# Graph attention layer on one core: the turned source ids leave PSUM through ScalarE instead of VectorE, and ScalarE instead of SyncE issues their way to DRAM

## The chip, the cores and the metric

The kernel runs on one core of one Trainium2 chip. The metric is the device time of one execution in microseconds (us), measured as the median of several runs. Engines are named as the profile names them: PE is TensorE, PEld its weight loads, DVE VectorE, ACT ScalarE, POOL GpSimd, SP SyncE. A q behind a name (SPq, ACTq) marks instructions of the engine's sequencer, such as the issue of a DMA.

## What is computed

A graph attention layer over 12,500 nodes with 128 features and 412,500 edges, whose targets are sorted. In the reference's terms (`src` and `dst` are the two rows of `edge_index`; the layer attends from `src` to `dst` and sums at `src`):

```
h, q, k, v = x@Wn+bn, x@Wq+bq, x@Wk+bk, x@Wv+bv;  eh = edge_attr@We+be
hmid   = leaky_relu(concat(q[src], k[dst], eh) @ A1 + b1, 0.2)
scores = leaky_relu(hmid @ A2 + b2, 0.2)
w      = softmax(scores.mean(-1), axis=0)          # over all edges
out    = segment_sum(w[:, None] * v[dst], src)
y      = gamma * layernorm(h + out) + beta
result = layernorm(x + y)
```

## The kernel before, in words

The edges arrive sorted by target, but the sums are by source, so the kernel sorts them by source on the chip, through DRAM. It has two kinds of work, which are interleaved in one written-out order.

**Making records** (`make`, lines 797 to 1020). The 403 groups of 1024 edges are cut into six parts. For each group PE multiplies one-hot matrices with rows of a key and value table (`rows`, L914 and L919), ACT takes the result out of PSUM into a record tile `rec` (L929, and L930 adds the source id within its block), and POOL scatters it to a table `rtab` in DRAM, with eight indirect DMAs a group (L941). There are six buffers for `rec`. Two tables `rtab` alternate between parts.

**Summing records** (`sums_of`, lines 1072 to 1407). When a part's records are all written, its 49 units, of two blocks of source nodes each and 14 or 12 tiles of 128 edges, are worked off while the next part is made: 294 units in all. The last part's units run with nothing left to make. The steps of one unit that matter here, with their lines:

- `load` (L1109): SP loads the unit's records, `rt`, 1.6 to 1.8 MB.
- `sources` (L1131): DVE reads the source ids out of `rt` into `sl`, a column for each tile.
- `turn` (L1139): PE turns `sl` into rows, into a PSUM tile named `psc`. There is one buffer of this name, and `scores` uses it too.
- `turned` (L1146): DVE takes the turned ids out of PSUM into bytes, `slT` (12 or 14 partitions of 128), clamping negative ones to 0.
- `put` (L1153): SP writes `slT` to a small DRAM tile `row` (1.5 or 1.8 KB).
- `spread` (L1158): SP reads `row` back, repeated over all 128 partitions, into `rowB`.
- `load_q` (L1120): SP loads the query rows `qs`.
- `onehot` (L1170): DVE compares `rowB` with each partition's number: the one-hot matrix `ohT`, in three or four pieces a unit.
- `hidden` (L1184, L1193), `sloped` (L1204, ACT) and `leaky` (L1208, DVE): the hidden layer `hm`; ACT writes the sloped copy and DVE takes the larger of the two.
- `scores` (L1221, PE, into `psc`), `above_zero` (L1235, ACT, a Relu out of PSUM into `z`), `heads` (L1247, PE), `maxima` (L1257, L1262, DVE), `maximum` (L1268, PE), `reference` (L1276, L1277, DVE).
- `weights` (L1286, ACT, needs `ref` of L1277), `select` (L1295, DVE), `weigh` (L1309, ACT, one instruction for a tile), `add` (L1338, PE).
- `lowered` (L1328, L1331, ACT), `before_it` (L1319, SP, loads `old`), `total` (L1354, DVE), `store` (L1361, SP, writes `atab`).

Nothing is scheduled by a planner at this point: `lags` and `last_lags` (lines 1044 to 1070) give for every step how many steps after the unit's own start it is recorded, and each engine executes its instructions in the recorded order. `turned` and `put` stand at the same step, two after `turn`; `spread` stands three steps later. An engine that waits for one instruction holds back everything behind it. SP also issues, in the same recorded order, the loads of the making part: `eat` (L808), `dstb` (L810), `kvs` (L826).

After the last unit a closing stage normalises the rows (lines 1410 to 1613).

Of the kernel before, what the change touches and what calls it, by code (L numbers as in the profile page):

```python
# [15 lines left out]
AF = mybir.ActivationFunctionType  # L16
ALU = mybir.AluOpType
# [4 lines left out]
P = 128  # L22
# [433 lines left out]
def sorted_path(  # L456
# [8 lines left out]
    nc = tc.nc  # L465
# [34 lines left out]
    for j, part in enumerate((1.0, -1.0)):  # L500
        nc.vector.tensor_scalar(
            A2s[:, H + 1 + j : H + 2 + j], A2s[:, H : H + 1], part * SLOPE / (1 - SLOPE), None,
            op0=ALU.mult,
# [6 lines left out]
    for j, part in enumerate((1.0, -1.0)):  # L510
        nc.vector.tensor_scalar(
            b2_r[:, H + 1 + j : H + 2 + j], b2_r[:, H : H + 1], part * SLOPE / (1 - SLOPE), None,
            op0=ALU.mult,
# [10 lines left out]
        out=signs, in_=signs, compare_op=ALU.not_equal, fill=SLOPE - 1, base=-(H + 2),  # L524
# [190 lines left out]
    def spans():  # L715
# [24 lines left out]
        out=above, in_=above, compare_op=ALU.is_gt, fill=0.0, base=0,  # L740
# [331 lines left out]
    def sums_of(bp):  # L1072
# [3 lines left out]
        for p, bs, t in units:  # L1076
            nt = len(bs) * t
# [65 lines left out]
        def turned(i):  # L1143
            st, nt = state[i], plans[i][0]
            st["slT"] = scp.tile([TM, P], U8, name="slT")
            nc.vector.tensor_scalar(  # L1146
                st["slT"][:nt, :], st.pop("pT")[:nt, :P], 0.0, None, op0=ALU.max
            )

        def put(i):  # L1150
            st, nt = state[i], plans[i][0]
            st["row"] = srow.tile([TM, P], U8, name="row")
            nc.sync.dma_start(out=st["row"][:nt, :], in_=st.pop("slT")[:nt, :])  # L1153

        def spread(i):
            st, nt = state[i], plans[i][0]
# [215 lines left out]
        for i, (nt, nk, s0, load_at, o) in enumerate(plans):  # L1372
            do(load_at, load, i)
            do(s0 + o["sources"], sources, i)
            do(s0 + o["turn"], turn, i)
            do(s0 + o["turned"], turned, i)
            do(s0 + o["turned"], put, i)
            do(s0 + o["spread"], spread, i)
            do(s0 + o["q"], load_q, i)
            for k, (c, c1) in enumerate(pieces(i)):  # L1380
                n, s = c1 - c, s0 + 2 * k
                do(s + o["onehot"], onehot, i, c, n, k)
                do(s, hidden, i, c, c, n, k)
                do(s + o["sloped"], sloped, i, c, c, n, k, late=1)
                do(s + o["leaky"], leaky, i, c, c, n, k, late=1)
            do(s0 + o["scores"], scores, i, 0, nt)
            do(s0 + o["above"], above_zero, i)
            do(s0 + o["heads"], heads, i, 0, nt)
            do(s0 + o["maxima"], maxima, i)
            do(s0 + o["maximum"], maximum, i, late=1)  # L1390
            do(s0 + o["reference"], reference, i)
            do(s0 + o["weights"], weights, i)
            do(s0 + o["old"], before_it, i)
            do(s0 + o["lowered"], lowered, i)
            for j, t0 in enumerate(range(0, nt, 4)):
                n = min(4, nt - t0)
                do(s0 + o["select"] + 2 * j, select, i, t0, n)
                do(s0 + o["weigh"] + 2 * j, weigh, i, t0, n)
                do(s0 + o["add"] + 2 * j, add, i, t0, n)
            do(s0 + o["total"], total, i)  # L1400
            do(s0 + o["store"], store, i)
# [328 lines left out]
    with tc.manual_schedule():  # L1730
        done = 0
        for p in range(NP + 1):
# [32 lines left out]
            tabs, made, nt = tables() if p == 0 else iter(()), 0, 1 + (2 * ng - 1) * (NB + 7) + ng  # L1765
# [99 lines left out]
```

## Time and profile before

| | us |
|---|---|
| median of 3 runs | 4985.54 (4974.44 to 4991.73) |
| the profiled execution | 4977.97 |
| its span, first to last instruction | 4976.3 |
| first and last `slT` (L1146) | 765.0 and 4810.6 |
| last indirect DMA of the records (L941) | 4395.4 |

The profiled execution is 7.6 us below the median; what lies around its span is 1.7 us. Four stretches are told apart in what follows, by what runs in them: up to 765 us the tables and the first part's records are made and no unit runs; from 765 to 3000 and from 3000 to 4396 units and records are interleaved; from 4396 to 4830 only the last part's units run; then the closing stage.

Wait rows read "engine, line waited for: total us, how often, the longest". A wait of several semaphores is put down to the one that came last by the profile. Rows of a window table give, for a stretch, its length and for each engine its busy time and instructions, then PE's granted clock, the share of the DMA engines and GB/s.

### The profile page before, as it was taken

The numbers are of one execution on the slowest core, as the hardware profiler recorded it, in microseconds if no ns is written. First come the engines' busy times: TensorE is split into PE (matmuls) and PEld (weight loads), VectorE is DVE, ScalarE is ACT, GpSimd is POOL, SyncE is SP. The second block draws the span as 40 slices with busy tenths as digits, with TensorE's granted clock in tenths as the row PEclk, the third lists the DMA queues.
The fourth block names the chain that finished last, engine by engine and source line by source line (L and its number), as shares of the span: only waits on it lengthen the run. The fifth ranks groups of instructions, "written<-read, shape, count | busy, mean of one in ns | idle before, by whom it ended". The sixth has DMA issues, their size and how long they took to land. (4 is left out here: it accounts for less than half of the span.)

```text
span 4976.3 us, 87101 instructions
## 1 busy us (share of the span) xinstructions
PE 4076.9 (82%) x27267; PEld 3176.9 (64%) x27568; DVE 4181.3 (84%) x9010; ACT 3168.0 (64%) x8326; POOL 3327.3 (67%) x3280
## 2 busy tenths in 40 slices
PE   3665547878888989988988888988889888889997
PEld 2444435666666766776766676776667666666786
DVE  7888867888888888888988887888889898877777
ACT  2442224655656777777777776777777666667785
POOL 3777777777777777777777777767667777731003
PEclk7787868999999999999999999999999999999999
DMA  5888978999888998888898888888888898889864
GB/s 187 285 288 272 369 246 300 317 318 307 275 280 295 315 310 308 311 307 299 315 308 310 303 310 280 306 303 307 297 297 302 300 312 304 298 289 308 302 238 171
DMA packets 603263, 1462.23 MB, mean 294 GB/s; under 512 B 103678, under 2 KB 329105, under 8 KB 600996
## 3 DMA queue, kind: packets, MB, share of 16 engines
q1 hardware_dynamic: 447696, 1027.15, 62.9%
q0 software_dynamic: 154752, 429.39, 22.7%
q8 instruction: 220, 3.60, 0.3%
q14 instruction: 255, 2.09, 0.1%
q10 hardware_dynamic: 340, 0.01, 0.0%
HBM read 884.13 MB, written 585.06 MB: 295 GB/s over the span
## 5 line engine op out<-in xcount | busy, mean ns | idle before, releaser
L941 POOL DMA_INDIRECT rtab<-rec,idx x3224 | 3242.7, 1006 | 1150.6 <-issue 783.3
L929 ACT ACTIVATE rec<-pkv 128x1024 f32<-128x1024 f32 x806 | 821.6, 1019 | 1162.7 <-PE pkv L919 519.1
L1309 ACT ACTIVATE ohw<-ohs,w 128x128 f32<-128x128 bf16 x3822 | 1256.1, 399 | 121.8 <-DVE ohs L1295 59.0
L1338 PE MATMUL psm<-rt,ohw 128*128 128x128 f32 x7644 | 1085.4, 285 | 3.4 <-ACT ohw L1309 0.8
L1338 PEld LDWEIGHTS psm<-rt,ohw 128*128 128x128 f32 x7644 | 997.7, 197 | 101.4 <-ACT hm L1204 13.0
L919 PE MATMUL pkv<-WeS,eat 128*128 128x256 f32 x3224 | 920.5, 412 | 0.0
L1208 DVE TENSOR_TENSOR hm<-ph,hm 128x512 f32<-128x512 f32 (+1 forms) x1029 | 662.5, 644 | 265.9 <-ACT hm L1204 261.2
L914 PE MATMUL pkv<-kvs,ohd 128*128 128x256 bf16 x3224 | 530.0, 291 | 290.5 <-ACT rec L929 283.0
L1184 PE MATMUL ph<-ident,rt 128*128 128x128 f32 x3822 | 625.4, 284 | 118.1 <-DVE hm L1208 112.9
L1170 DVE TENSOR_SCALAR ohT<-rowB,iotaP,power 128x512 bf16<-128x512 uint8 (+2 forms) x1176 | 598.0, 519 | 93.0 <-DMA rowB<-row 92.7
L914 PEld LDWEIGHTS <-ohd 128*128 128x128 bf16 x3224 | 317.0, 103 | 540.6 <-issue 423.4
L919 PEld LDWEIGHTS pkv<-WeS,eat 128*128 128x128 f32 x3224 | 606.4, 209 | 70.2
L1184 PEld LDWEIGHTS ph<-ident,rt 128*128 128x128 f32 x3822 | 442.2, 146 | 323.9 <-issue 144.9
L1204 ACT ACTIVATE hm<-ph 128x512 f32<-128x512 f32 (+1 forms) x1029 | 567.0, 551 | 33.8 <-PE ph L1193 26.8
L857 DVE TENSOR_SCALAR ohd<-dstb,node 128x1152 bf16<-128x1152 uint8 x404 | 564.9, 1398 | 0.0
L1193 PE MATMUL ph<-ohT,qs 128*128 128x512 bf16 (+2 forms) x2051 | 531.6, 340 | 29.2 <-DVE ohT L1170 14.5
L883 DVE TENSOR_TENSOR ats<-pc,oh 128x792 f32<-128x792 f32 x403 | 391.1, 970 | 37.1 <-PE pc L865 37.1
L1221 PE MATMUL psc<-hm,A2s 128*32 128x384 f32 (+2 forms) x2352 | 360.0, 550 | 63.1 <-DVE hm L1208 34.4
L1295 DVE TENSOR_TENSOR ohs<-iotaE,sl 128x512 bf16<-128x512 bf16 (+1 forms) x1029 | 409.1, 398 | 1.0 <-ACT ohw L1309 1.0
L847 DVE TENSOR_REDUCE few<-oh 128x99 bf16<-128x792 bf16 x403 | 395.1, 980 | 13.9
L894 DVE TENSOR_REDUCE pos<-ats 128x8 f32<-128x792 f32 x403 | 389.1, 966 | 1.7
L1247 PE MATMUL psm<-headsum,z 128*128 128x4 f32 (+1 forms) x2058 | 256.7, 245 | 58.0 <-DVE part L1354 50.8
(192 smaller groups left out, 3876.2 us busy)
## 6 DMA issues: line engine op xcount, KB each, us to landing
rt<-rtab SPq DMA_DIRECT2D x147, 1820.0 KB
rt<-rtab SPq DMA_DIRECT2D x147, 1560.0 KB
eat<-in_ea SPq DMA_DIRECT2D x201, 512.0 KB
rtab<-rec,idx POOLq DMA_INDIRECT x3224
dstb<-dtab SPq DMA_DIRECT2D x201, 256.0 KB
rtab<-empty SPq DMA_DIRECT2D x76, 520.0 KB
qs<-qtab SPq DMA_DIRECT2D x294, 128.0 KB
atab<-part SPq DMA_DIRECT2D x294, 128.0 KB
```

The costliest lines, as they stand in the source:

```text
L857: nc.vector.tensor_scalar(to, ids[:, cols], node, None, op0=ALU.is_equal)
L914: nc.tensor.matmul(pk[:, i, h, :], ohd[t], kvs, start=(h == 0), stop=False,)
L919: nc.tensor.matmul(pk[:, i, :, :D], eat[:, (j + i) * P : (j + i + 1) * P], WeS, start=False, stop=True,)
L929: nc.scalar.activation(rec[:, :, :, : 2 * D], pk, AF.Copy)
L941: one_tile = nc.gpsimd.indirect_dma_start(out=rtab[p % TABS][:, :], out_offset=bass.IndirectOffsetOnAxis(ap=idxs[g][:, t : t + 1], axis=0) ...
L1170: nc.vector.tensor_scalar(st["oh"][k][:, (a - t0) * P : (b - t0) * P], st["rowB"][:, a * P : b * P], iotaP, power[:, bs[u] : bs[u] + 1], o ...
L1184: nc.tensor.matmul(ph[:, j * P : (j + 1) * P], st["rt"][:, t0 + j, :D], ident, is_transpose=True, start=(j == 0), stop=False,)
L1193: nc.tensor.matmul(ph[:, cols], st["qs"][:, j0 // t, s, :], oh[:, cols], start=False, stop=(s == 1 and j1 == t0 + n),)
L1204: nc.scalar.activation(hm, state[i]["ph", k][:, : n * P], AF.Copy, scale=SLOPE)
L1208: nc.vector.tensor_tensor(hm, ph[:, : n * P], hm, op=ALU.max)
L1309: nc.scalar.activation(ohw[:, j, :], ohs[:, :, j], AF.Copy, scale=st["w"][:, t0 + j : t0 + j + 1])
L1338: nc.tensor.matmul(st["psS"][:, (1 + u) * P : (2 + u) * P], ohw[:, j, :], st["rt"][:, t0 + j, D : 2 * D], start=(k == 0), stop=(k == t - 1),)
```

## The change

`turned` becomes a Relu on ACT in place of the maximum with 0 on DVE, and `put` is issued from ACT's queue in place of SP's. `spread` stays on SP. The lags, the buffers and the transfers themselves stay as they are.

```
         def turned(i):
             st, nt = state[i], plans[i][0]
             st["slT"] = scp.tile([TM, P], U8, name="slT")
-            nc.vector.tensor_scalar(
-                st["slT"][:nt, :], st.pop("pT")[:nt, :P], 0.0, None, op0=ALU.max
-            )
+            nc.scalar.activation(st["slT"][:nt, :], st.pop("pT")[:nt, :P], AF.Relu)

         def put(i):
             st, nt = state[i], plans[i][0]
             st["row"] = srow.tile([TM, P], U8, name="row")
-            nc.sync.dma_start(out=st["row"][:nt, :], in_=st.pop("slT")[:nt, :])
+            nc.scalar.dma_start(out=st["row"][:nt, :], in_=st.pop("slT")[:nt, :])
```

The changed file is two lines shorter, so that from here on its lines are two lower (L1309 becomes L1307, and so on).

ACT, a unit of 14 tiles among those that run while records are made. Before:

```order
L929 ACTIVATE rec<-pkv 128x4x256
L930 ACTIVATE rec<-srcl 128x4x4
L1328 ACTIVATE by<-refs,ref 128x2
L1331 ACTIVATE refs<-ref 128x2
L1309 ACTIVATE ohw<-ohs,w 128x128 x4
L1204 ACTIVATE hm<-ph 128x384
L929 ACTIVATE rec<-pkv 128x4x256
L930 ACTIVATE rec<-srcl 128x4x4
L1309 ACTIVATE ohw<-ohs,w 128x128 x2
L1204 ACTIVATE hm<-ph 128x512
```

And with the change, at the same place:

```order
L929 ACTIVATE rec<-pkv 128x4x256
L930 ACTIVATE rec<-srcl 128x4x4
L1326 ACTIVATE by<-refs,ref 128x2
L1329 ACTIVATE refs<-ref 128x2
L1307 ACTIVATE ohw<-ohs,w 128x128 x4
L1146 ACTIVATE slT<-psc 14x128
L1151 DMA row<-slT 14x128
L1202 ACTIVATE hm<-ph 128x384
L929 ACTIVATE rec<-pkv 128x4x256
L930 ACTIVATE rec<-srcl 128x4x4
L1307 ACTIVATE ohw<-ohs,w 128x128 x2
L1202 ACTIVATE hm<-ph 128x512
```

The two new instructions stand between four weighings of one unit and the sloped copy of another, with an evacuation of records behind them.

ACT again, among the last part's units, of 12 tiles, from one unit's `lowered` to the next unit's weighing. Before:

```order
L1328 ACTIVATE by<-refs,ref 128x2
L1331 ACTIVATE refs<-ref 128x2
L1309 ACTIVATE ohw<-ohs,w 128x128 x4
L1204 ACTIVATE hm<-ph 128x512
L1286 ACTIVATE w,sums<-S,ref 128x12
L1309 ACTIVATE ohw<-ohs,w 128x128 x4
```

And with the change:

```order
L1326 ACTIVATE by<-refs,ref 128x2
L1329 ACTIVATE refs<-ref 128x2
L1307 ACTIVATE ohw<-ohs,w 128x128 x4
L1202 ACTIVATE hm<-ph 128x512
L1146 ACTIVATE slT<-psc 12x128
L1151 DMA row<-slT 12x128
L1284 ACTIVATE w,sums<-S,ref 128x12
L1307 ACTIVATE ohw<-ohs,w 128x128 x4
```

Here they stand just ahead of the weights `w`, which need DVE's `ref`.

SP, one round of the last part's units. Before:

```order
L1158 DMA rowB<-row 128x1536
L1361 DMA atab_73<-part 128x256
L1153 DMA row<-slT 12x128
L1109 DMA rt<-rtab_75 128x2x1560
L1120 DMA qs<-qtab 128x512
L1319 DMA old<-atab_72 128x256
L1158 DMA rowB<-row 128x1536
```

And with the change:

```order
L1156 DMA rowB<-row 128x1536
L1359 DMA atab_73<-part 128x256
L1109 DMA rt<-rtab_75 128x2x1560
L1120 DMA qs<-qtab 128x512
L1317 DMA old<-atab_72 128x256
L1156 DMA rowB<-row 128x1536
```

The put is gone from SP; the loads `rt`, `qs` and `old` that stood behind it follow the store directly, and the next instruction on SP that has to do with the ids is `rowB`, which needs the landed `row`.

## The prediction

> **What bounds the kernel now.** I read the windows of the four stretches first, then who waits for whom in each, and last the timeline around single units. The windows, with PE, PEld, DVE, ACT and POOL in this order:
>
> ```profile
> core 0: us, PE busy (x) PEld busy (x) DVE busy (x) ACT busy (x) POOL busy (x), PEclk, DMA share, GB/s
> 0.00:765.00 765.00, 406.93 (x1562) 284.64 (x1563) 608.37 (x1015) 233.24 (x323) 546.67 (x522) 0.76 0.81 275
> 765.00:3000.00 2235.00, 1926.07 (x13174) 1506.99 (x13321) 1935.85 (x4019) 1520.89 (x4025) 1710.07 (x1722) 0.96 0.89 305
> 3000.00:4396.00 1396.00, 1232.24 (x8582) 967.44 (x8685) 1203.52 (x2637) 990.79 (x2685) 988.02 (x996) 0.96 0.88 301
> 4396.00:4830.00 434.00, 402.08 (x3097) 314.35 (x3148) 329.10 (x924) 334.29 (x1036) 30.22 (x15) 0.99 0.83 285
> ```
>
> POOL does not look like the bound, with 1710 of 2235 us busy, until its idle time is read:
>
> ```profile
> POOL rtab L941 <- issue: 783.3, 2568, 0.6
> ```
>
> Between two indirect DMAs it loses 783.3/2568 = 0.305 us to nothing that another engine does. So from 765 to 3000, where POOL runs its records alone, a record costs 1710.07/1722 + 0.305 = 1.298 us, and 1722 of them 2235 us: all of the stretch. **Stretch A (765 to 3000) is bound by POOL**, which the change does not touch; ACT, with 1521 of 2235 us busy, must only keep six `rec` buffers ahead. **Stretch B (3000 to 4396)** is not: 996 x (0.992 + 0.305) = 1292 us of 1396, so 104 us are lost to something else, and that is the most that can be won there. **Stretch C (4396 to 4830)** has no records, and PE is busy 402 of 434 us: about 32 us are to be won at most. Ahead of 765 no unit runs, and behind 4830 no `slT` is made:
>
> ```profile
> L1146 DVE TENSOR_SCALAR slT<-psc x294: 265/272/279, 765.0 to 4810.6; 12x128 uint8<-12x128 f32 x74, 14x128 uint8<-14x128 f32 x73
> ```
>
> So only B and C, 1830 us with 149 of the 294 units, can move:
>
> ```profile
> 3000.00:4396.00 1396.00, 27.00 (x99) 0.96 0.88 301
> 4396.00:4830.00 434.00, 13.59 (x50) 0.99 0.83 285
> ```
>
> These are the windows of L1146 alone: 99 and 50 units, 27.0 and 13.6 us of DVE. In B no single engine is full (PE 88%, DVE 86%, ACT 71%); they wait for each other. The waits of DVE there, then of ACT, PE and POOL:
>
> ```profile
> DVE hm L1208 <- ACT hm L1204: 71.9, 68, 2.6
> DVE sl L1131 <- DMA rt<-rtab: 49.1, 33, 5.8
> DVE ohT L1170 <- DMA rowB<-row: 34.2, 21, 5.5
> ```
>
> ```profile
> ACT rec L929 <- PE pkv L919: 162.0, 79, 8.8
> ACT w L1286 <- DVE ref L1277: 134.8, 69, 4.3
> ```
>
> ```profile
> PE psc L1221 <- DVE slT L1146: 13.8, 10, 5.1
> ```
>
> ```profile
> POOL rtab L941 <- ACT rec L930: 54.9, 34, 6.9
> ```
>
> And of SP in B:
>
> ```profile
> SPq L1158 <- DMA row<-slT: 382.3, 95, 8.9
> SPq L1153 <- DVE slT L1146: 334.1, 75, 7.2
> SPq L1153 <- DVE ohT L1170: 115.1, 23, 7.6
> ```
>
> SP stands still at the put for 449 us and at the spread for 382 more, of 1396. That would be free if nothing behind it were late, but DVE waits 83 us for two loads, `rt` and `rowB`, that SP issues behind these two waits. In C the same, DVE's row first, then ACT's, then SP's:
>
> ```profile
> DVE ohT L1170 <- DMA rowB<-row: 33.8, 27, 7.6
> ```
>
> ```profile
> ACT w L1286 <- DVE ref L1277: 88.7, 51, 9.1
> ```
>
> ```profile
> SPq L1153 <- DVE slT L1146: 150.4, 36, 6.2
> SPq L1153 <- DMA rt<-rtab: 39.0, 13, 4.0
> ```
>
> **The change part by part: what ACT pays.** No Relu of 128 columns is in the trace; the nearest is `z`, also a Relu out of PSUM:
>
> ```profile
> L1235 ACT ACTIVATE z<-psc,b_c 128x384 f32<-128x384 f32 x147 | 82.4, 561 | 0.0
> L1328 ACT ACTIVATE by<-refs,ref 128x2 f32<-128x2 f32 x245 | 70.2, 287 | 0.0
> L1235 ACT ACTIVATE z<-psc,b_c 32x256 f32<-32x256 f32 x147 | 68.5, 466 | 1.9
> ```
>
> 128 columns fewer are 95 ns fewer, so 128 columns take about 371 ns; the bounds are 287 (two columns) and 466 (256). The put cost SP 362 ns, and ACT issued two small transfers at the program's start:
>
> ```profile
> L1153 SPq DMA_DIRECT2D row<-slT x294: 315/362/794, 765.3 to 4810.9; - x147
> ```
>
> ```profile
> L508 ACTq DMA_DIRECT2D b_r<-in_b x1: 520/520/520, 1.5 to 1.5; - x1
> ```
>
> ```profile
> L517 ACTq DMA_DIRECT2D b_d<-b_r x1: 234/234/234, 4.7 to 4.7; - x1
> ```
>
> I take 362, between 234 and 794. The put must wait until `slT` is written, so ACT cannot overlap it with the Relu, nor the next instruction with the Relu's end; I add 0.13 us for that, an estimate from the 0.1 us by which rows of ACT's timeline below overlap. **0.86 us a unit**: 85 us in B, 43 in C; at the bounds 0.52 to 1.39. The Trainium skill, "ScalarE: Activation LUTs", Rules for kernel authors, says of relu and max "Use VectorE, not ScalarE". Its formulas give an estimate of 293 ns with immediate operands or 387 with a pointer for the bias, by which the sum below would be -47 or -45 us in place of -45. By the rule alone the change goes the wrong way, as the second rival has it; the trace sets against it that DVE is the fuller engine here (1204 against 991 us in B).
>
> In C the pair stands in a gap. PE's turn of a unit, ACT's rows behind it, and DVE's `slT` of that unit:
>
> ```profile
> 4643.87 0.22 PE L1139 MATMUL psc<-identB,sl 128*12 128x128 bf16 x1
> ```
>
> ```profile
> 4645.55 0.59 ACT L1204 ACTIVATE hm<-ph 128x512 f32<-128x512 f32 x1
> 4649.24 0.30 ACT L1286 ACTIVATE w<-S,ref 128x12 f32<-128x12 f32 x1 [3.10 <-DVE ref L1277]
> ```
>
> ```profile
> 4649.58 0.27 DVE L1146 TENSOR_SCALAR slT<-psc 12x128 uint8<-12x128 f32 x1
> ```
>
> ACT is idle from 4646.14 on and could have had `slT` 3.4 us earlier than DVE. Over C this gap is 88.7/51 = 1.74 us on average, twice the 0.86: I charge one unit in ten, 4 us. If that cover is gone, it is all 43.
>
> In B the place is behind four `ohw`. One unit, ACT and DVE, and then one the other way round:
>
> ```profile
> 3620.84 0.47 ACT L1204 ACTIVATE hm<-ph 128x384 f32<-128x384 f32 x1
> 3621.21 1.00 ACT L929 ACTIVATE rec<-pkv 128x1024 f32<-128x1024 f32 x1
> ...
> 3623.55 0.71 ACT L1309 ACTIVATE ohw<-ohs,w 128x128 f32<-128x128 bf16 x2 [1.23 <-DVE S L1257]
> ```
>
> ```profile
> 3623.65 0.28 DVE L1146 TENSOR_SCALAR slT<-psc 14x128 uint8<-14x128 f32 x1
> ```
>
> ```profile
> 3156.65 0.47 ACT L1204 ACTIVATE hm<-ph 128x384 f32<-128x384 f32 x1
> ```
>
> ```profile
> 3154.54 0.28 DVE L1146 TENSOR_SCALAR slT<-psc 14x128 uint8<-14x128 f32 x1
> ```
>
> In the first, ACT comes to the place 2.8 us ahead of DVE, and its wait of 1.23 us behind it swallows the 0.86. In the second it comes 2.1 us behind DVE. So in B the put is sooner in some units and later in others. What covers the cost is ACT's waiting, 162.0 + 134.8 = 297 us against 85. It is not covered where DVE already waits for the sloped copy, 68 times among some 99 x 3.5 copies (L1204 has 1029 for 294 units), a fifth: I charge 0.2 x 85 = 17 us.
>
> **What DVE and SP gain.** DVE loses 27.0 us of work in B and 13.6 in C. It is the fuller of the two engines in B, but PE's 88% stands behind it, so I count half: 13 and 7. SP no longer waits at the put. It runs on to `rowB` and waits there for the landed `row`, so the loads between the two go out earlier, and behind `rowB` `rt` goes out earlier by what the spread gains. The wait for the landing does not vanish, it takes over part of the put's. I count half of the `rowB` waits, 17 us in B and 17 in C, and a quarter of the `rt` waits in B, 12. PE's 13.8 us for `slT` are not added: they are the same lateness, seen from the single `psc` buffer. Bounds: below, no `rowB` or `rt` wait is saved; above, all 83 us in B, cut off at the 104, and 32 in C.
>
> **The sum.** A: 0. B: -13 - 17 - 12 + 17 = -25. C: -17 - 7 + 4 = -20. Together -45 us on the profiled 4978, which is 4933; the median shown lies 7.6 us above that execution, so 4941. What is late next: in C PE, which the -20 leaves with 12 us of idle time; in B ACT's `rec` behind PE's `pkv`.
>
> **Rivals.** *The landing stays.* SP's 382 us at the spread show that the way through DRAM, not the issue, may be what is long. Then the spread goes out no sooner, the `rowB` and `rt` terms fall away, and what stays is -20 for DVE and +21 for ACT: about 4986. For it speaks that a landing takes 382.3/95 = 4.0 us of SP's time even after the put; against it, that SP's 334 and 150 us at the put are not landing time, and that in C ACT is free 3.4 us sooner. The Trainium skill, "DMA: Bandwidth & Descriptors", Issuing engines are not separate DMA queues, says that another issuing engine saves only the issue time. By that rule this rival is what comes; its section on queues has the 16 engines take turns between rings, which would speak for a sooner landing. No row here decides.
>
> *ACT becomes the one waited for.* The put stands still in ACT's stream, and the sloped copy, the evacuation and the weights queue behind it; DVE, PE and POOL (its 54.9 us for `rec` in B) wait for those. The put can also wait for an older transfer: 13 times in C it did so on SP for `rt`, 3.0 us each, which on ACT would stop compute. Price: of 128 us in B and C three quarters uncovered, +96, with the 66 us of gains halved: +63, or 5049. It decides when more than half of the cost is uncovered (66/128). Against it: the gap in C and ACT's 297 us of waits in B. In A POOL's pace hides either way.
>
> **How the numbers follow.** The forecast, 4905 to 4970 around 4941, gets 0.50; the landing rival, 4970 to 5000, 0.21; ACT, 5000 to 5060, 0.26; a gain near the ceilings, below 4905, 0.03. Leaving out half of ACT's and what lies below, the range is 4895 to 5028. About 0.3%, 15 us, is what a measurement of this kernel tells from none: faster 0.53, same 0.21, slower 0.26.
>
> **What would show it.** Right: the waits of SP at L1153 gone, those at the spread not grown by as much, DVE's `rowB` rows in B and C below half, DVE's 40.6 us gone, POOL unchanged in A and idle less in B, ACT's wait for `ref` in C shorter by the pair. Wrong: DVE's wait for `hm` in B well above 90 us, POOL's for `rec` above 55, a pair on ACT of over 1.4 us, or POOL falling off its pace in A.

## The result and the profile after

The median went from 4985.54 to **4919.0 us** (4917.37 to 4926.41 in 3 runs); the ratio of the two kernels is 0.9885, 95% [0.9867, 0.9903]. (The two medians alone give 0.9867; in the later sessions the medians of the kernel before were 4977.24 to 4978.78, so 4985.54 is on the high side.) The forecast was 4941. The profiled execution took 4926.41 us, its span 4924.5, which is 51.8 us less than the span before. The sum of the forecast was -45 on that profile, so in size it is close; but it was put together from B -25 and C -20, and the trace says otherwise:

| | before | after | difference | forecast |
|---|---|---|---|---|
| record 2230 of 3224 (3001.2 us before) | 3001.2 | 2999.9 | -1.4 | 0 |
| last record (L941) | 4395.4 | 4346.4 | -49.0 | -25 |
| from there to the last unit's weights `w` | 441.3 | 439.6 | -1.7 | -20 |

These are the starts of the same instruction in both traces. **All of the gain is made in stretch B, and none in C.** From here on B ends at the last record, and C is what lies from there to the last unit's `w`. Differences of a few us between two single profiles are not read. In e2_dve_given_back and e9_rt_on_act below, one of five executions was slow, at a lower granted clock (13225.61 us at 0.399 and 6391.71 us at 0.559); their medians count it, their ratios do not.

The windows of the changed kernel, columns as before, cut at its own end of B (4347 in place of 4396):

```profile
core 0: us, PE busy (x) PEld busy (x) DVE busy (x) ACT busy (x) POOL busy (x), PEclk, DMA share, GB/s
...
765.00:3000.00 2235.00, 1922.19 (x13183) 1502.43 (x13330) 1909.58 (x3878) 1552.37 (x4169) 1710.05 (x1722) 0.96 0.89 305
3000.00:4347.00 1347.00, 1217.91 (x8576) 962.43 (x8678) 1184.31 (x2532) 1009.08 (x2783) 988.53 (x995) 0.97 0.91 311
4347.00:4781.00 434.00, 408.49 (x3103) 316.56 (x3152) 319.22 (x877) 342.27 (x1085) 29.81 (x15) 0.99 0.82 285
```

In A, POOL has the same 1722 records in the same time, so nothing of the change shows there. B is 49 us shorter with the same work in it. C is as long as it was: 434 us. The two new instructions cost ACT less than was estimated; the columns are minimum, median and maximum in ns:

```profile
L1146 ACT ACTIVATE slT<-psc x294: 249/250/252, 764.1 to 4758.5; 12x128 uint8<-12x128 f32 x74, 14x128 uint8<-14x128 f32 x73
L1151 ACTq DMA_DIRECT2D row<-slT x294: 295/312/353, 764.3 to 4758.8; - x147
```

So 0.56 us a unit and 0.03 between them (0.86 was forecast). The waits in B, of DVE, POOL and SP, to be laid beside those of before:

```profile
DVE hm L1206 <- ACT hm L1202: 84.1, 82, 2.8
DVE sl L1131 <- DMA rt<-rtab: 34.9, 21, 5.2
...
DVE ohT L1168 <- DMA rowB<-row: 7.8, 6, 4.0
```

```profile
POOL rtab L941 <- ACT rec L930: 40.5, 38, 3.8
```

```profile
SPq L1156 <- DMA row<-slT: 672.9, 93, 11.7
```

DVE's waits for `rt` and `rowB` fell from 83.3 to 42.7 us: 40.6 of the 49. SP stood 831 us at put and spread together, and stands 673 now. The same rows in C:

```profile
DVE ohT L1168 <- DMA rowB<-row: 38.1, 28, 7.6
```

```profile
SPq L1156 <- DMA row<-slT: 92.0, 20, 8.5
SPq L1120 <- DMA rt<-rtab: 44.1, 14, 4.4
SPq L1109 <- DMA row<-slT: 32.9, 12, 4.4
```

In C DVE waits for `rowB` no less than before (33.8). The last row is odd: the load `rt` (L1109) reads nothing of the ids, and yet waits for their landing. In the trace the transfers of SP and ACT share eight completion semaphores (101 to 108), given out in turn in the recorded order, and each waits until the one that had its semaphore before has landed: the put issued at 4606.29 us and the load `rt` issued at 4610.61 both have 108. So a put that lands late holds loads that have nothing to do with it.

### The profile page after: what moved, and what is told of

Same layout as the page of the kernel before. It is cut to its first block, busy times and chain, and to the rows that moved or that the text cites. A ratio compares the mean times of both kernels' runs of the same rounds, so it can differ in the third digit from the quotient of the medians.

```text
span 4924.5 us, 87125 instructions
## 1 busy us (share of the span) xinstructions
PE 4054.9 (82%) x27267; PEld 3162.5 (64%) x27568; DVE 4128.2 (84%) x8716; ACT 3226.3 (66%) x8620; POOL 3328.9 (68%) x3280
## 5 line engine op out<-in xcount | busy, mean ns | idle before, releaser
L941 POOL DMA_INDIRECT rtab<-rec,idx x3224 | 3244.3, 1006 | 1099.6 <-issue 767.0
L1307 ACT ACTIVATE ohw<-ohs,w 128x128 f32<-128x128 bf16 x3822 | 1256.2, 399 | 70.8 <-DVE ohs L1293 35.2
```

The costliest lines, as they stand in the source:

```text
L941: one_tile = nc.gpsimd.indirect_dma_start(out=rtab[p % TABS][:, :], out_offset=bass.IndirectOffsetOnAxis(ap=idxs[g][:, t : t + 1], axis=0) ...
L1307: nc.scalar.activation(ohw[:, j, :], ohs[:, :, j], AF.Copy, scale=st["w"][:, t0 + j : t0 + j + 1])
```

## The experiments

Theory 1, from these rows: in B the gain is that SP's stream no longer stands at the put; in C the put now comes behind `rt` instead of ahead of it. Rivals: DVE's relief makes the gain; the ids land sooner because of the queue they travel in; ACT's cost is hidden or not. Beside the stretches, one more number is read from the issue times in the traces: from the end of a put to the start of its spread (**put to spread**), which is the landing wherever SP stands there. Beside it stands the landing itself, from the end of a put's issue to the end of its last packet in the trace (**landed**). Both are means in us over all units of B (99) and C (50):

| kernel | put from, Relu on | last record | C | put to spread B, C | landed B, C | SP stands at put + spread, B | DVE waits for rt + rowB, B |
|---|---|---|---|---|---|---|---|
| before | SP, DVE | 4395.4 | 441.3 | 5.40, 2.63 | 4.50, 1.58 | 831 | 83.3 |
| the change | ACT, ACT | 4346.4 | 439.6 | 4.66, 5.38 | 3.66, 4.08 | 673 | 42.7 |
| e1_relu_only | SP, ACT | 4391.6 | 427.5 | 6.30, 2.71 | 5.37, 1.68 | 867 | 89.2 |
| e3_put_only | ACT, DVE | 4353.6 | 459.4 | 4.63, 4.99 | 3.62, 4.03 | 727 | 45.4 |
| e7_put_twice | ACT and SP, ACT | 4345.5 | 446.0 | 4.68, 4.70 | 3.42, 2.65 | 692 | 40.3 |
| e8_put_by_stage | ACT, in C SP; ACT | 4341.9 | 427.7 | 4.59, 2.72 | 3.57, 1.61 | 680 | 39.1 |
| e9_rt_on_act | SP, ACT | 4387.6 | 484.3 | 5.10, 5.93 | 4.09, 5.27 | 882 | 106.0 |

**e1_relu_only**: the change without the second half.

```
-            nc.scalar.dma_start(out=st["row"][:nt, :], in_=st.pop("slT")[:nt, :])
+            nc.sync.dma_start(out=st["row"][:nt, :], in_=st.pop("slT")[:nt, :])
```

> Relu on ScalarE, put still issued by SyncE. Theory (SP released): the gain of the change comes from SP no longer standing still at the put, so here only DVE's relief is left: 15 to 25 us below before, SP's wait at the put stays at some 800 to 1000 us in all, DVE's wait for rowB in B stays near 34 us. Rival (DVE relieved): the gain is the 27 us of work that DVE loses in B and what hangs on it: 45 to 65 us below before, as the whole change.

4959.41 us, ratio 0.9963 [0.995, 0.9975]. The size is as expected, 19.4 us below the 4978.78 of the kernel before beside it, but not by the expected way: the gain is in C, 13.8 us. The last record comes 3.8 sooner, and record 2230 was that much sooner already, so B gains nothing. DVE's wait for `rowB` in C, 33.8 us before:

```profile
DVE ohT L1168 <- DMA rowB<-row: 15.7, 10, 7.7
```

With the ids turned by ACT and the put still SP's, that wait halves, as the forecast had it for the whole change.

**e2_dve_given_back**: the change, with DVE doing something as long at the old place.

```
+            idle = scp.tile([TM, P], U8, name="idle")
+            nc.vector.tensor_scalar(idle[:nt, :], ident[:nt, :], 0.0, None, op0=ALU.max)
```

> The change, and beside it a DVE instruction of the same shape (14x128 or 12x128 into bytes) at the old place, from a constant in SBUF into a tile that nobody reads. Theory (SP released): 5 to 25 us above the change, so still 40 to 60 us below before. Rival (DVE relieved): the gain goes, 50 us or more above the change.

```profile
L1148 DVE TENSOR_SCALAR idle<-ident x294: 200/206/470, 764.6 to 4768.2; 12x128 uint8<-12x128 f32 x74, 14x128 uint8<-14x128 f32 x73
```

4929.69 us, ratio 0.9892 [0.9874, 0.991]. 206 of the 272 ns are back on DVE, and of the 51.8 us between the profiles 43.7 stay. Of the 8 us, 5 are there at record 2230, ahead of B; the last record comes 6.2 later than with the change. So DVE's relief is the small part of the gain in B: about 8 us at the most, if 6.2 is scaled from 206 ns to 272.

**e3_put_only**: `turned` stays a maximum on DVE, the put is ACT's.

> DVE keeps taking the ids out of PSUM, ScalarE issues the put and must wait for DVE there. Theory (SP released): SP gains what it gains in the change, but ScalarE stands still for DVE wherever it is ahead (3.4 us in the unit of C that the prediction shows): between 20 us below and 20 us above before. Rival (DVE relieved): nothing is won and ScalarE loses: 10 to 60 us above before.

4956.23 us, ratio 0.9958 [0.9944, 0.9972]: 22.6 us below the kernel before beside it, a little more than the theory allowed. The put alone wins 41.8 us in B, nearly all that the change wins, and loses 18.1 in C. So the two edits work in different stretches: the put makes B, the Relu would make C, and the put takes that back.

**e4_relu_twice**: the change, with a second Relu of the same ids behind the first, into a tile that nobody reads.

```
-            nc.scalar.activation(st["slT"][:nt, :], st.pop("pT")[:nt, :P], AF.Relu)
+            nc.scalar.activation(st["slT"][:nt, :], st["pT"][:nt, :P], AF.Relu)
+            again = scp.tile([TM, P], U8, name="again")
+            nc.scalar.activation(again[:nt, :], st.pop("pT")[:nt, :P], AF.Relu)
```

> The change with the Relu done a second time into a tile that nobody reads, 0.25 us more of ScalarE for each of the 294 units (25 us in B, 12 in C). If ScalarE's cost is hidden by its waits, as the prediction charged: 0 to 8 us above the change. If ScalarE is the one waited for: 25 to 40 us above the change.

```profile
L1148 ACT ACTIVATE again<-psc x294: 250/250/252, 767.8 to 4754.9; 12x128 uint8<-12x128 f32 x74, 14x128 uint8<-14x128 f32 x73
```

4921.9 us, ratio 0.9885 [0.9869, 0.9901]: 250 ns more a unit, 37 us in B and C, cost nothing that can be told. ACT has room for this much more work, so the work that the change gives it is most likely covered too; no run measures that part alone.

**e7_put_twice**: the change, and at SP's old place a second copy into a DRAM tile that nobody reads.

```
-            nc.scalar.dma_start(out=st["row"][:nt, :], in_=st.pop("slT")[:nt, :])
+            hold = srow.tile([TM, P], U8, name="hold")
+            nc.scalar.dma_start(out=st["row"][:nt, :], in_=st["slT"][:nt, :])
+            nc.sync.dma_start(out=hold[:nt, :], in_=st.pop("slT")[:nt, :])
```

> The change, and at the put's old place in SP's stream a second copy of the ids to a DRAM tile that nobody reads, so that SP stands still for slT as before while the ids that are used still travel from ACT's queue. Theory 1, what B wins is that SP's stream no longer stands at the put: the win in B goes, the last record comes at 4380 to 4396, and C gets back the 14 us that the put on SP had with the Relu on ACT, because rt is again held behind the ids; ratio about 0.996. Rival, the ids land sooner from a queue of their own and that is what B wins: the last record stays at 4346 within 10 us and C stays at -2; ratio about 0.989.

4931.22 us, ratio 0.9906 [0.9889, 0.9922]. SP's rows and DVE's in B (lines from here on two higher, as before the change):

```profile
SPq L1153 <- ACT slT L1146: 426.7, 98, 7.8
SPq L1158 <- DMA row<-slT: 265.2, 85, 5.3
```

```profile
DVE sl L1131 <- DMA rt<-rtab: 30.3, 18, 5.2
...
DVE ohT L1170 <- DMA rowB<-row: 10.0, 5, 4.7
```

SP stands at the put again, 426.7 us, and the win in B stays whole. **Theory 1 falls for B.** 426.7 + 265.2 are 692, the 673 of the change over again: one stretch of waiting, from the idle SP to the landed ids, cut in two at another place. What did change is how soon the ids land: 3.42 us after the put's issue, 4.50 before. In C neither forecast came, 446.0 us in place of about 426 or 439; this run says little there, because the second copy takes a turn of the eight semaphores too, and SP goes on to the spread 2.05 us after the landing, against 1.29 in the change.

**e9_rt_on_act**: e1_relu_only, with the load of the records (L1109) issued from ACT, so that the put on SP no longer shares its queue with it.

```
-            nc.sync.dma_start(
+            nc.scalar.dma_start(
                 out=rt[:, :n, :].rearrange("p (u t) w -> p u (t w)", u=m),
```

> The Relu on ACT, the put on SP, and the records' load rt (1.6 to 1.8 MB) issued from ACT in place of SP. With the second copy the win in B did not hang on SP standing at the put. Theory now: a put in SP's queue lands behind the loads that SP issued ahead of it, rt above all (in B it goes out 5.5 us ahead of the put; put to spread takes 6.3 us with the put on SP and 4.7 with the put on ACT), and in C lands soon (2.7 us) because rt goes out 0.45 us behind it. Then here, with rt in the other queue, put to spread falls in B to 4.3 to 5.0 us though the put is still SP's. In C it grows above 3.5 us where rt now goes out ahead of the put, and stays at 2.7 where it doesn't. Rival: it is the issuing engine (ACT's transfers are served sooner while records are made), and B stays at 6.0 or more. ACT also waits for rt's buffer now, so the time as a whole says little: ratio 0.99 to 1.01.

5013.05 us, ratio 1.007 [1.0048, 1.0092]; the time is lost because `rt` now stands in ACT's stream, and DVE waits for it:

```profile
DVE sl L1131 <- DMA rt<-rtab: 99.8, 61, 4.5
...
DVE ohT L1168 <- DMA rowB<-row: 6.2, 6, 2.3
```

Put to spread fell from 6.30 to 5.10 in B, though the put is still SP's: not the issuing engine counts, but what else is in its queue. (DVE's wait for `rowB`, 30.8 us in e1_relu_only, is 6.2 here, but the late `rt` may hide a part of it. 5.10 is 0.1 over what was expected; `rt` goes out 4.4 us ahead of the put here, 5.5 in e1_relu_only.) In C it grew from 2.71 to 5.93, where `rt` now goes out 2.5 us ahead of the put on average instead of 0.48 behind it. Sorted by how long before the put the last `rt` was issued, the units of B give the medians of put to spread:

| | rt under 4.5 us ahead | 4.5 to 8 | over 8 |
|---|---|---|---|
| put and rt both on SP (e1_relu_only) | 7.29 (33 units) | 5.58 (61) | 3.24 (5) |
| the same, before | 6.26 (17) | 5.57 (64) | 3.91 (18) |
| put on ACT, rt on SP (the change) | 4.71 (13) | 4.67 (71) | 4.13 (15) |
| put on SP, rt on ACT (e9_rt_on_act) | 5.05 (57) | 4.47 (41) | 3.62 (1) |

In SP's queue the put lands when what is ahead of it is nearly through; from another queue the distance hardly counts. The packets show it: with `rt` under 4.5 us ahead, the put's last packet came after the last one of `rt` (1.6 or 1.8 MB) in 25 of the 33 units of e1_relu_only (8 of 17 before), and in 1 of 13 with the change. `rt` is not all that stands ahead: SP's queue also holds `eat`, `dstb` and `kvs` (512, 256 and 64 KB), which stay there in e9_rt_on_act and may be why it landed at 4.09 us and the change at 3.66. It also explains why the Relu alone gave so little in B: the put went out 0.8 us sooner behind `rt` (5.5 against 6.3 us) and took 0.9 us longer to land. One unit of B in both kernels, one of the slowest of e1_relu_only, SP's issues in e1_relu_only first, then SP's and ACT's in the change (start, duration):

```profile
3666.49 0.37 SPq L1109 DMA_DIRECT2D rt<-rtab  x1
...
3672.72 0.36 SPq L1151 DMA_DIRECT2D row<-slT  x1
3673.13 0.35 SPq L1120 DMA_DIRECT2D qs<-qtab  x1
3682.79 0.32 SPq L1156 DMA_DIRECT2D rowB<-row  x1
```

```profile
3643.18 0.37 SPq L1109 DMA_DIRECT2D rt<-rtab  x1
...
3654.97 0.32 SPq L1156 DMA_DIRECT2D rowB<-row  x1
```

```profile
3649.41 0.31 ACTq L1151 DMA_DIRECT2D row<-slT  x1
```

In both the put follows `rt` by 6.23 us. In SP's queue the spread starts 9.71 us after the put's end, with the put in ACT's 5.25. Between `rt` and the put SP issued five transfers in both, `old`, `eat`, `dstb`, `kvs` and `atab`, 1.1 MB (and `qs` in the change). By the packets, `rt` was through at 3677.29 us in e1_relu_only and the put at 3682.08, behind these five as well; in the change `rt` was through at 3653.01 and the put at 3653.66, ahead of most of them.

**e8_put_by_stage**: the put from ACT while records are made, from SP for the last part's 49 units.

```
-            nc.scalar.dma_start(out=st["row"][:nt, :], in_=st.pop("slT")[:nt, :])
+            issuer = nc.sync if units[i][0] == NP - 1 else nc.scalar
+            issuer.dma_start(out=st["row"][:nt, :], in_=st.pop("slT")[:nt, :])
```

> The Relu on ACT throughout, the put from ACT while records are made and from SP for the last part's 49 units. If the effects of the two edits add up stage by stage as the runs with one edit each say (B -49, C -13 to -14), the last record comes at 4346 within 8 us, C takes about 421 us instead of 434, and the ratio is 0.986, faster than the change by 10 to 12 us. Rival, C's loss with the put on ACT is not the put's place but a debt that a shorter B leaves (rt of the last part's units loaded later in relation to their work): C stays at 432 to 434 us and the ratio at 0.989.

**4902.06 us, ratio 0.9849 [0.9834, 0.9863]**: faster than both kernels, with B as in the change and C at 427.7, which is 13.6 less than before (the expected 421 counts from 434, so it too is 13 less). Stage by stage the effects add up, and the rival, a debt left by a shorter B, falls. C in the change, SP and ACT, and then SP in this kernel:

```profile
4594.00 0.38 SPq L1109 DMA_DIRECT2D rt<-rtab  x1
...
4595.41 0.74 SPq L1156 DMA_DIRECT2D rowB<-row  x1
...
4596.73 0.42 SPq L1109 DMA_DIRECT2D rt<-rtab  x1
```

```profile
4597.25 0.30 ACTq L1151 DMA_DIRECT2D row<-slT  x1
```

```profile
4599.55 0.32 SPq L1152 DMA_DIRECT2D row<-slT  x1
4599.96 0.37 SPq L1109 DMA_DIRECT2D rt<-rtab  x1
4600.38 0.46 SPq L1120 DMA_DIRECT2D qs<-qtab  x1
...
4602.07 0.51 SPq L1157 DMA_DIRECT2D rowB<-row  x1
```

In the change `rt` is out 0.5 us ahead of the ids. With the put on SP its wait for `slT` also holds `rt` back behind it, and the spread goes out 2.2 us after the put's end. That the ids themselves land later, and not only SP is held by a semaphore, the packets show: 4.08 us after the put's issue in C of the change, 1.61 here. In 17 of the 50 units of the change `rt` was over 8 us ahead and put to spread was still 5.43 (median); what holds those was not worked out. DVE's wait for `rowB` in C:

```profile
DVE ohT L1169 <- DMA rowB<-row: 15.6, 10, 8.3
```

**e5_spread_on_act**: the change, with the spread from ACT as well.

```
-            nc.sync.dma_start(
+            nc.scalar.dma_start(
                 out=st["rowB"][:, : nt * P],
```

> The change, with the spread (rowB) issued from ACT as well, so that SP stands at neither of the two and ACT stands at the landing. If what is left to win in B is SP's standing at the spread (672.9 us there with the change), DVE's 34.9 us for rt in B fall below 10, and the last record comes 20 us or more ahead of the change's 4346. If the landing itself is what costs, ACT takes over the standing: ACT rows at L1156 of 200 us or more in B, DVE's wait for hm well above 84 us, and the last record later than the change's by 30 us or more. I expect the second, ratio to before 0.992 to 1.005.

4976.53 us, ratio 0.9993 [0.998, 1.0006]: the whole gain is gone. SP stands at neither transfer now, and DVE hardly waits for `rt`; but it waits for the others:

```profile
DVE hm L1206 <- ACT hm L1202: 99.8, 99, 3.0
DVE ohT L1168 <- DMA rowB<-row: 62.8, 35, 5.3
...
DVE sl L1131 <- DMA rt<-rtab: 9.3, 5, 3.0
```

The 200 us that ACT was expected to wait at the spread do not show: from the end of the instruction ahead to the start of the spread the timeline gives 93 us in B, in 49 of 98 units. How much of the 43 us in B is this standing, and how much the later `rowB`, stays open.

**e6_spread_later** (`spread=-turn + 4 + 2 * e` in `lags`, one step later) and **e10_turned_sooner** (e8_put_by_stage with `turned=-turn + e`, one step sooner) try to take the landing off SP's path.

> The change, with the spread one step later while records are made (C is as in the change). If SP's standing at the spread delays rt, its 672.9 us in B fall by a third or more, DVE's 34.9 us for rt with it, and the last record comes 5 to 20 us sooner than 4346. If rowB is already only just in time, DVE's 7.8 us for rowB in B grow to 30 or more and the last record comes 5 to 20 us later. Ratio 0.985 by the first, 0.992 by the second.

4923.27 us, ratio 0.9895 [0.9878, 0.9912]: no difference from the change that can be told. SP's 672.9 us fell to 616.6, not by a third; DVE's waits moved from `rt` (25.7) to `rowB` (13.7).

> The version with the put from ACT while records are made and from SP in the last part, with the Relu and the put one step sooner while records are made, right behind the step of PE's turn. If the landing of the ids is what still costs in B (SP stands 680 us at the spread, DVE 33 for rt behind it), the standing falls below 400 us, the rt waits below 20, and the last record comes 5 to 20 us sooner than 4342; ratio 0.981 to 0.984. Rival: ACT then comes to the Relu before PE has turned the ids and stands for it, with the sloped copies behind: DVE's wait for hm grows by 20 us or more, and the last record is the same or later; ratio 0.985 to 0.990.

4903.94 us, ratio 0.985 [0.9831, 0.987]: the same as e8_put_by_stage. SP, then DVE, in B:

```profile
SPq L1157 <- DMA row<-slT: 572.6, 89, 10.5
```

```profile
DVE hm L1207 <- ACT hm L1203: 98.8, 96, 2.8
DVE sl L1131 <- DMA rt<-rtab: 20.5, 16, 4.2
```

Neither theory is met: SP's standing stays above 400, the `rt` waits fall by 9 us, and DVE's wait for `hm` grows by 16. The last record comes 5 us sooner, which two single profiles do not tell from nothing. What is won at the one seems to be given back at the other.

## Why the prediction held, and where it did not

- **A, no change: right.** POOL's pace set it before and after (record 2230 at -1.4 us).
- **B, -25: the right sign and the right waits, too small.** The `rowB` and `rt` terms were -17 and -12; the rows fell by 26.4 and 14.2, together -41. The step "I count half" of the `rowB` waits and "a quarter" of the `rt` waits was mis-sized; ACT's +17 is most likely near 0 (e4_relu_twice), and DVE's -13 not more than about 8 (e2_dve_given_back). The reason given, "SP no longer waits at the put", was wrong: e7_put_twice keeps that wait and keeps the gain. What falls is the landing, in another queue than `rt`'s (4.50 to 3.66 us). No run changes the landing and nothing else: that it makes the gain rests on the rivals that fell, on DVE's rows, and on the packets.
- **C, -20: failed.** The step was that the put's lateness goes and half of the `rowB` waits with it, -17, DVE's -7 and ACT's +4; measured -1.7. The earlier Relu is worth -13.8 (e1_relu_only, with 18 us less of `rowB` waits, so the half was right), but the put in ACT's queue takes it back: +18.1 alone (e3_put_only). The two orders of SP in the section on the change show it: the put stood ahead of `rt`, and once it is gone `rt` goes out first. I read there only that loads go out sooner, not that 1.6 MB then meet the ids on the way; e8_put_by_stage restores the order and the gain. ACT's wait for `ref`, which was to be shorter by the pair (0.59 us in 50 units), fell from 88.7 to 81.9.
- **ACT's price, 0.86 us a unit:** 0.59. The 371 ns estimated for the Relu from `z` were 250. That any of it is paid does not show. DVE's wait for `hm` grew from 71.9 to 84.1, below the 90 set as the mark.
- **The rival that the landing stays** is refuted in B and true in C, for a reason that it did not name. The Trainium skill, "DMA: Bandwidth & Descriptors", Issuing engines are not separate DMA queues, says that another issuing engine saves only the time to initiate a transfer. Here that time is 0.36 us a unit on SP, 36 us over the 99 units of B, and the put's move is worth 41.8. But e7_put_twice, where SP still issues a copy in every unit, keeps the gain, and in C the move costs 18.1 us: the rule misses what the queue does to a small transfer among large ones. The same page's Queues, rings and completion order (SP and ACT each have rings of their own, consumed in order, between which the 16 engines take turns) agrees with the 7.29 against 4.71 us close behind `rt`.
- **The rival that ACT becomes the one waited for** is refuted for the change as far as the Relu's time goes by e4_relu_twice; POOL's wait for `rec` fell from 54.9 to 40.5 us, where it was to rise.

Two errors of opposite sign, B too small by 24 us and C too large by 18, left the sum nearly right. That the time came out so close is luck: of the two stretches that were to move, C did not, and B moved in another way than was thought.

## What to carry to other kernels

Before moving a small transfer to another queue, read what was issued just ahead of it and just behind it in the old one: in this kernel it gained where it stood behind a large load, and lost its place where it stood ahead of one. Moving it also lets what stood behind it go first, and this can differ by stage, so choose the queue by stage. The time that an engine stands at two dependent transfers, a put and the read behind it, is best read as one number (831 and 673 us here); that the first wait goes says nothing until the landing is shown to come sooner.

## What the runs showed of the hardware

- How soon 1.5 or 1.8 KB land from SP's queue depends on what is ahead. Put to spread in B (e1_relu_only, medians): 3.24 us with `rt` more than 8 us ahead (5 units), 7.29 with `rt` less than 4.5 us ahead (33 units); from the other queue, in the change, 4.13 to 4.71. A queue of its own is no free road either: 5.38 us on average in C of the change, where `rt` went out on SP less than 4.5 us ahead in 33 of 50 units.
- A Relu of 12 or 14 partitions by 128 columns from PSUM into bytes takes ACT 250 ns, DVE's maximum of the same 272. The issue of the put takes ACT 312 ns, SP 362 (medians).
